# Four changes around the attention layer of a four-layer graph network: where skip terms, keys and row sums are kept and when they move

## The chip, the cores and the metric

The kernel runs on one core of one Trainium2 chip. The metric is the time of one execution on the device in microseconds (us), from the first to the last instruction; the number given for a kernel is the median of several executions. Engines are named as in the profile: PE is the matrix engine, PEld its weight loads, DVE the vector engine, ACT the scalar engine, POOL the general-purpose engine, SP the engine that here only starts transfers. DMA stands for the 16 transfer engines that the core's queues share.

## The reference, cut to what matters

Four graph layers follow one another on 4096 nodes with 128 features each, all with the same dense 4096 x 4096 matrix `adj` of zeros and ones (about 64 ones in a row). After each layer, `x = layernorm(x + layer(x, adj))`. The change concerns the second, an attention with four heads of 32 channels, gated with a linear skip term:

```python
def _L1_gnn_ref(x, adj, Wq, bq, Wk, bk, Wv, bv, Ws, bs, Wb):   # H = 4 heads, C = 32
    q = (x @ Wq + bq).reshape(n, H, C)
    k = (x @ Wk + bk).reshape(n, H, C)
    v = (x @ Wv + bv).reshape(n, H, C)
    attn = jnp.einsum('nhc,mhc->hnm', q, k) / np.float32(np.sqrt(C))
    neg = jnp.where((adj == 0.0)[None], -jnp.inf, attn)
    e = jnp.where(mask[None], 0.0, jnp.exp(neg - m))             # m: row maximum
    alpha = e / denom
    out = jnp.einsum('hnm,mhc->hnc', alpha, v)                   # then transposed to (n, C*H)
    x_r = x @ Ws + bs                                            # the skip term
    beta = jax.nn.sigmoid(jnp.concatenate([out, x_r, out - x_r], axis=-1) @ Wb)
    return beta * x_r + (1.0 - beta) * out
```

The third layer needs the row sums of `adj` (the degrees): `deg = jnp.sum(adj_hat, axis=1)`. The kernel computes them during the second layer, in time that ACT has left there.

## The kernel before

The first layer writes the transposed matrix to DRAM as `adjT`, in 8 x 8 tiles of 128 x 4 x 512 numbers (1 MB each). The second layer has a preparation and a loop.

The preparation makes q and k, 512 nodes at a time. Each is split into a rounded part and a rest (`cut`), written to the DRAM tensor `qk`, and read back into another arrangement of partitions: `KS` for all keys, `QS` for 512 queries. `stack` issues these reads from POOL, four of 256 KB for each piece of 512 nodes. Then the values (`V`, a view of `VA`) and the skip terms get their biases.

```python
            rd = self.dram.tile([P, NT, D], F32, tag="rd", name="rd")
            ...
            def stack(a, dst, c):
                for r, part in enumerate(((0, 1, 0, 1), (0, 0, 1, 1))[a]):
                    nc.gpsimd.dma_start(out=dst[r * C : (r + 1) * C, :, :],
                        in_=qk[a, part, :, c * S : (c + 1) * S].rearrange("(h c) n -> c h n", h=NH))
            ...
                for c in range(NC):                              # 8 pieces
                    for a, w, bias in ((1, wk, bkc), (0, wq, bqc)):
                        p = self.ps_t.tile([P, S], F32, tag="pt", name="pqk")
                        nc.tensor.matmul(p, lhsT=w, rhs=XT[:, s], start=True, stop=True)
                        cut = rot.tile([P, 2, S], F32R, tag="cut", name="cut", bufs=9)
                        nc.scalar.activation(cut[:, 0, :], p, AF.Identity, bias=bias)         # L822
                        nc.vector.scalar_tensor_tensor(cut[:, 1, :], p, bias, ...)            # L823
                        nc.vector.tensor_reduce(mx[:, a, c : c + 1], ...)                     # L826
                        nc.sync.dma_start(out=qk[a, :, :, s]..., in_=cut.bitcast(F32))        # L829
                        if c < 2:
                            stack(a, (QS[c], KS[:, :, s])[a], c)
                for g in self.groups():                          # 8 groups of 4 row blocks: values
                    ...
                    for k, t in enumerate(g):
                        nc.vector.tensor_tensor(V[:, t, :, 0:C], p[:, k, :]..., bvr..., ALU.add)   # L837
                for g in self.groups():                          # skip terms
                    ...
                    r = rot.tile([P, 4, D], F32, tag="r", name="r", bufs=4)
                    nc.vector.tensor_tensor(r, p, bsr.unsqueeze(1).to_broadcast([P, 4, D]), ALU.add)  # L848
                    nc.sync.dma_start(out=rd[:, g[0] : g[-1] + 1, :], in_=r)                  # L849
                ...                                              # a bound on |q||k| -> fi
            small = nc.values_load(fi, min_val=0, max_val=1)
            with tc.If(small > 0) as cmp:
                self.attention_unshifted(VA, KS, QS, at0, stack, rd, wb)   # taken with these inputs
```

The loop runs over 8 tiles of 512 queries (`I`), and in each over 32 blocks of 128 keys (`jb`). One block is four score matmuls (`scores`: PE L909, ACT exponential L916, DVE mask L918) and, two blocks later in the program, eight PE instructions that sum values (`sums`: L935). `load` fetches an `adjT` tile for every four blocks. `row` fetches half a row block of `adj` (1 MB) into the single buffer `nat`, and `degree` sums it along the row on ACT and fetches the next. `ending` finishes a query tile during the first blocks of the next.

```python
            rot = ctx.enter_context(tc.tile_pool(name="rotf", bufs=1))
            atp = ctx.enter_context(tc.tile_pool(name="atf", bufs=2))
            ep = ctx.enter_context(tc.tile_pool(name="ef", bufs=3))
            ...
            def degree(n):
                i, k = halves[n]
                nat = st["nat"]
                nc.scalar.activation(nat, nat, AF.Identity, accum_out=self.deg2[:, k, i : i + 1])  # L901
                row(n + 1)                                       # L894, issued by ACT
            ...
                load(0, 1)
                row(0)
                for n in range(-LEAD, len(seq)):                 # LEAD = 2
                    if n + LEAD < len(seq):
                        I, jb = seq[n + LEAD]
                        if jb % 4 == 0:
                            ...
                                load(m // NT, m % NT // 4)
                        if jb % 4 == 3:
                            degree(8 * I + jb // 4)
                        if I == 0 and jb % 4 == 0 and jb // 4 + 2 < NS:
                            c = jb // 4 + 2
                            stack(1, KS[:, :, c * S : (c + 1) * S], c)
                        if jb == 3 and 0 < I < NS - 1:
                            stack(0, QS[(I + 1) % 2], I + 1)
                        scores(I, jb)
                    if n >= 0:
                        I, jb = seq[n]
                        sums(I, jb)
                        next(rest, None)                         # a step of ending(I - 1)
```

Of the kernel before, what the change touches and what calls it, by code (L numbers as in the profile page):

```python
# [9 lines left out]
F32 = mybir.dt.float32  # L10
F32R = mybir.dt.float32r
AF = mybir.ActivationFunctionType
ALU = mybir.AluOpType
# [3 lines left out]
P = 128  # L17
# [7 lines left out]
S = 512  # L25
# [5 lines left out]
class Net:  # L31
# [3 lines left out]
    def __init__(self, ctx, tc, x, adj):  # L35
        self.tc, self.nc, self.adj = tc, tc.nc, adj
        self.N, self.D = x.shape
        self.NT = self.N // P
        self.MM = min(512, self.N)
        self.const = ctx.enter_context(tc.tile_pool(name="const", bufs=1))  # L40
        self.feat = ctx.enter_context(tc.tile_pool(name="feat", bufs=1))
        self.wtp = ctx.enter_context(tc.tile_pool(name="wtp", bufs=3))
        self.ident = self.const.tile([P, P], F32, tag="ident", name="ident")
        make_identity(self.nc, self.ident)

        self.XA = self.feat.tile([P, self.NT, self.D + 1], F32, tag="X", name="X")
# [722 lines left out]
    def layer1(self, Wq, bq, Wk, bk, Wv, bv, Ws, bs, Wb):  # L769
# [3 lines left out]
        NH, C = 4, D // 4  # L773
        with ExitStack() as ctx:
# [10 lines left out]
            qk = self.dram.tile([2, 2, P, N], F32, tag="qk", name="qk")  # L785
            rd = self.dram.tile([P, NT, D], F32, tag="rd", name="rd")
            wb = [self.load_row(Wb[k * D : (k + 1) * D, 0], f"wb{k}") for k in range(3)]
# [17 lines left out]
            with ExitStack() as pctx:  # L805
# [10 lines left out]
                for c in range(NC):  # L816
                    s = slice(c * S, (c + 1) * S)
                    for a, w, bias in ((1, wk, bkc), (0, wq, bqc)):
                        p = self.ps_t.tile([P, S], F32, tag="pt", name="pqk")
                        nc.tensor.matmul(p, lhsT=w, rhs=XT[:, s], start=True, stop=True)  # L820
                        cut = rot.tile([P, 2, S], F32R, tag="cut", name="cut", bufs=9)
                        nc.scalar.activation(cut[:, 0, :], p, AF.Identity, bias=bias)  # L822
# [9 lines left out]
                for g in self.groups():  # L832
                    p = self.ps_t.tile([P, 4, P], F32, tag="pt", name="pt")
                    for k, t in enumerate(g):
                        nc.tensor.matmul(p[:, k, :], lhsT=XT[:, t * P : (t + 1) * P], rhs=wv, start=True, stop=True)
                    for k, t in enumerate(g):
                        nc.vector.tensor_tensor(  # L837
                            V[:, t, :, 0:C],
                            p[:, k, :].rearrange("p (h c) -> p h c", h=NH),
                            bvr.rearrange("p (h c) -> p h c", h=NH),  # L840
                            ALU.add,
                        )
                for g in self.groups():
                    p = self.ps_t.tile([P, 4, P], F32, tag="pt", name="pt")
                    for k, t in enumerate(g):
                        nc.tensor.matmul(p[:, k, :], lhsT=XT[:, t * P : (t + 1) * P], rhs=ws, start=True, stop=True)
                    r = rot.tile([P, 4, D], F32, tag="r", name="r", bufs=4)
                    nc.vector.tensor_tensor(r, p, bsr.unsqueeze(1).to_broadcast([P, 4, D]), ALU.add)  # L848
                    nc.sync.dma_start(out=rd[:, g[0] : g[-1] + 1, :], in_=r)  # L849

# [13 lines left out]
            with tc.If(small > 0) as cmp:  # L864
                self.attention_unshifted(VA, KS, QS, at0, stack, rd, wb)
            with cmp.Else():
                self.attention_shifted(V, qk, rd, wb)

    def attention_unshifted(self, VA, KS, QS, at0, stack, rd, wb):

# [3 lines left out]
        with ExitStack() as ctx:  # L874
            rot = ctx.enter_context(tc.tile_pool(name="rotf", bufs=1))
            atp = ctx.enter_context(tc.tile_pool(name="atf", bufs=2))
            ep = ctx.enter_context(tc.tile_pool(name="ef", bufs=3))
            ps_s = ctx.enter_context(tc.tile_pool(name="ps_s", bufs=3, space=PSUM))
            ps_v = ctx.enter_context(tc.tile_pool(name="ps_v", bufs=1, space=PSUM))
            st = {("at", 0, 0): at0}  # L880

            def load(I, J):
                at = atp.tile([P, 4, S], F32, tag="at", name="at")
                nc.sync.dma_start(out=at, in_=self.adjT[I, J])
                st["at", I, J] = at

            halves = [(i, k) for i in range(NT) for k in range(2)]

            def row(n):

                if n < len(halves):
                    i, k = halves[n]
                    st["nat"] = rot.tile([P, N // 2], F32, tag="nat", name="nat")
                    nc.scalar.dma_start(  # L894
                        out=st["nat"], in_=self.adj[i * P : (i + 1) * P, k * N // 2 : (k + 1) * N // 2]
                    )

            def degree(n):
                i, k = halves[n]
# [44 lines left out]
            def ending(I):  # L944

                ev = rot.tile([P, 2, S], F32, tag="ev", name="ev")
                for a in range(2):
                    nc.scalar.copy(ev[:, a, :], st["po"][a])
                r = rot.tile([P, 4, D], F32, tag="r", name="r")
                o = rot.tile([P, 4, D], F32, tag="o", name="o")  # L950
# [3 lines left out]
                yield  # L954
                nc.sync.dma_start(out=r, in_=rd[:, 4 * I : 4 * I + 4, :])
                for a in range(2):
# [48 lines left out]
            with tc.manual_schedule():  # L1005
# [3 lines left out]
                for n in range(-LEAD, len(seq)):  # L1009
# [26 lines left out]

    def attention_shifted(self, V, qk, rd, wb):

# [3 lines left out]
        with ExitStack() as ctx:  # L1042
# [3 lines left out]
            KT = keep.tile([P, N], F32, tag="KT", name="KT")  # L1046
            K2 = keep.tile([P, S], F32, tag="K2", name="K2")
            for c in range(N // S):
# [8 lines left out]
            nc.gpsimd.memset(QH, 0.0)  # L1057
            Q2 = keep.tile([P, 2, P], F32, tag="Q2", name="Q2")
            work = ctx.enter_context(tc.tile_pool(name="work1", bufs=1))
            self.on_scalar = 0  # L1060

            for i in range(NT):
# [56 lines left out]
                o = self.wtp.tile([P, D], F32, tag="o", name="o")  # L1119
                r = self.wtp.tile([P, D], F32, tag="r", name="r")  # L1120
                nc.sync.dma_start(out=r, in_=rd[:, i, :])
                nc.scalar.copy(junk[:, 2, :], po)
# [326 lines left out]
```

## Time and profile before

| | |
|---|---|
| time, median of 3 executions | 2413.66 us (2411.61 to 2417.61) |
| profiled execution, span | 2421.0 us |
| mean granted PE clock | 0.912 |
| busy: PE, DVE, ACT, POOL | 84%, 79%, 60%, 4% of the span |
| HBM read, written | 371.20 MB, 79.72 MB |
| first layer (from the timeline) | up to about 981 us |
| second layer, preparation | about 981 to 1031 us |
| second layer, loop | about 1031 to 1875 us |
| third and fourth layers | about 1875 us to the end |

The profile is of one execution. Busy time counts an engine's instructions, not the starting of transfers. The windows view gives, for stretches of the span, each engine's busy time with its number of instructions, then the granted PE clock (1.00 is full speed), the busy share of the DMA engines (it can pass 1 where transfers of several queues overlap) and the rate in GB/s. The waits view lists who waited for whom: total us, number of times, the longest one. The chain is followed back from the last instruction, at each step to what released it; its lines give start, length and what it was. The timeline gives start, length, engine, line and operation, with the idle time before it in brackets. A line such as L916 is a line of the kernel.

### The profile page before, as it was taken

How to read it: one execution, taken by the hardware profiler on the slowest of the kernel's cores; microseconds unless marked ns; L12 is line 12 of the kernel's file. 1: busy time of each engine (PE TensorE's matmuls, PEld its weight loads, DVE VectorE, ACT ScalarE, POOL GpSimd, SP SyncE). 2: the span in 40 equal slices, each digit the busy share in tenths (PEclk: the TensorE clock that was granted, in tenths of full speed). 3: DMA queues.
4: the chain of work that ended last, by engine and by line, in shares of the span. 5: the costliest groups of instructions: out<-in, count | busy, mean ns of one | idle time of the engine just before them, and what ended most of it. 6: DMA issues, size and time to landing. Idle time of an engine off the chain costs nothing.

```text
span 2421.0 us, 24184 instructions
## 1 busy us (share of the span) xinstructions
PE 2028.3 (84%) x8795; PEld 1117.9 (46%) x8795; DVE 1900.7 (79%) x2719; ACT 1459.7 (60%) x1761; POOL 100.7 (4%) x141
## 2 busy tenths in 40 slices
PE   5477878778777771789999999999997899979998
PEld 4266666566666660433333333333332444444443
DVE  6478788788788888757877878878787877568887
ACT  5688888898888886368777787877775000010000
POOL 2000000000000042210000000000000000000000
PEclk7689889889898885789999999999999899979999
DMA  2456465464646530796464655646444788528884
GB/s 53 134 181 204 146 204 199 159 207 154 203 170 191 190 111 1 264 245 200 163 195 143 194 170 166 195 164 187 160 166 171 280 290 284 187 110 294 287 288 169
DMA packets 115174, 452.66 MB, mean 187 GB/s; under 512 B 10016, under 2 KB 20320, under 8 KB 74080
## 3 DMA queue, kind: packets, MB, share of 16 engines
q1 hardware_dynamic: 87248, 298.90, 36.4%
q10 hardware_dynamic: 18576, 135.27, 16.0%
q0 software_dynamic: 9216, 16.78, 3.9%
q8 instruction: 73, 1.20, 0.2%
q14 instruction: 61, 0.50, 0.1%
HBM read 371.20 MB, written 79.72 MB: 186 GB/s over the span
## 4 chain that ended last, share of the span: by engine, by line
PE 56%; DVE 25%; ACT 12%; DMA 3%; issue 3%; ACTq 0%; SPq 0%; POOL 0%; DVEq 0%; POOLq 0%
PE pv L935 14%; PE pa L1324 9%; PE pa L1179 9%; PE ps L909 8%; DVE e L918 5%; PE pz L583 4%; DVE w L606 3%; PE pi L674 3%; DVE t L632 3%; DVE w L636 3%; PE ptA L564 3%; ACT t L628 3%; ACT at L572 2%; ACT e L916 2%; DMA nat<-in_adj_dram 2%
## 5 line engine op out<-in xcount | busy, mean ns | idle before, releaser
L918 DVE SCALAR_TENSOR_TENSOR e<-at,e 128x2048 f32<-128x2048 f32 x256 | 581.4, 2287 | 183.1 <-ACT e L916 183.1
L916 ACT ACTIVATE e<-ps 128x1024 f32<-128x1024 f32 x512 | 489.3, 1025 | 137.5 <-PE ps L909 102.7
L935 PE MATMUL pv<-e,VA 128*64 128x512 f32 x2048 | 505.9, 616 | 7.8 <-DVE e L918 7.5
L909 PE MATMUL ps<-QS,KS 128*128 128x512 f32 x1024 | 317.4, 429 | 41.5 <-ACT e L916 32.9
L909 PEld LDWEIGHTS ps<-QS,KS 128*128 128x128 f32 x1024 | 173.3, 191 | 270.8 <-ACT e L916 177.1
L674 PE MATMUL pi<-HA,w 128*128 128x129 f32 x1152 | 184.6, 334 | 84.1 <-DVE w L636 84.1
L935 PEld LDWEIGHTS pv<-e,VA 128*64 128x64 f32 x2048 | 126.6, 138 | 256.2 <-issue 230.3
L1324 PE MATMUL pa<-w,F 128*128 128x512 f32 x512 | 224.0, 598 | 13.3 <-DVE w L1321 13.3
L1179 PE MATMUL pa<-at,Y 128*128 128x512 f32 x512 | 223.0, 596 | 0.0
L674 PEld LDWEIGHTS pi<-HA,w 128*128 128x128 f32 x1152 | 177.7, 247 | 94.3 <-DVE w L636 94.3
L1321 DVE SCALAR_TENSOR_TENSOR w<-rho,col,at 128x512 f32<-128x512 f32 x256 | 186.7, 746 | 19.7 <-PE pa L1324 2.5
L591 DVE SCALAR_TENSOR_TENSOR t<-ei,de,pz 128x512 f32<-128x512 f32 x144 | 107.3, 747 | 111.4 <-PE pz L583 107.9
L564 PE MATMUL ptA<-ident,ad 128*128 128x128 f32 x1032 | 146.6, 288 | 41.4 <-ACT at L572 34.0
L1189 DVE SCALAR_TENSOR_TENSOR odd<-at 128x2048 f32<-128x2048 f32 x64 | 146.6, 2290 | 38.2 <-DMA at<-adjT 37.6
L564 PEld LDWEIGHTS ptA<-ident,ad 128*128 128x128 f32 x1032 | 125.7, 149 | 99.1 <-ACT at L572 51.3
L572 ACT COPY at<-ptA 128x512 f32<-128x512 f32 x200 | 108.4, 587 | 103.1 <-PE ptA L564 99.1
L583 PE MATMUL pz<-HT 128*128 128x512 f32 x292 | 166.3, 682 | 4.3 <-DVE w L655 4.0
L1324 PEld LDWEIGHTS pa<-w,F 128*128 128x128 f32 x512 | 97.6, 192 | 135.3 <-issue 100.6
L1179 PEld LDWEIGHTS pa<-at,Y 128*128 128x128 f32 x512 | 97.5, 192 | 119.8 <-issue 118.9
L606 DVE TENSOR_TENSOR w<-w,at 128x2048 f32<-128x2048 f32 x64 | 143.7, 2281 | 0.0
L1328 ACT COPY a<-pa 128x512 f32<-128x512 f32 x8 | 4.7, 586 | 206.8 <-PE pa L1324 206.8
L901 ACT ACTIVATE nat<-nat 128x2048 f32<-128x2048 f32 x64 | 122.7, 1918 | 11.1 <-DMA nat<-in_adj_dram 11.1
(340 smaller groups left out, 2370.0 us busy)
## 6 DMA issues: line engine op xcount, KB each, us to landing
at<-adjT SPq DMA_DIRECT2D x127, 1024.0 KB, 4.8
at<-adjT ACTq DMA_DIRECT2D x65, 1024.0 KB, 4.8
ad<-in_adj_dram SPq DMA_DIRECT2D x64, 1024.0 KB, 6.5
adjT<-at SPq DMA_DIRECT2D x64, 1024.0 KB, 8.4
nat<-in_adj_dram ACTq DMA_DIRECT2D x64, 1024.0 KB, 4.9
qk<-cut SPq DMA_DIRECT2D x16, 512.0 KB, 13.3
KS<-qk POOLq DMA_DIRECT2D x32, 256.0 KB, 11.1
QS<-qk POOLq DMA_DIRECT2D x32, 256.0 KB, 8.7
```

The costliest lines, as they stand in the source:

```text
L564: nc.tensor.transpose(pt[:, ib, :], st[p]["ad"][k][:, ib, jb * P : (jb + 1) * P], self.ident)
L572: copy(st[p]["at"][k][:, jb, :], st[p]["pt"].pop(m))
L583: nc.tensor.matmul(pz, lhsT=HT[:, j * P : (j + 1) * P], rhs=HT[:, I * S : (I + 1) * S], start=True, stop=True)
L606: nc.vector.tensor_tensor(w, w, at, ALU.mult)
L674: nc.tensor.matmul(self.po[ib // 2][:, ib % 2, :], lhsT=w[0][:, jb, ib * P : (ib + 1) * P], rhs=HA[:, 4 * J + jb, :], start=False, stop=(J ...
L909: nc.tensor.matmul(p[:, h, :], lhsT=KS[:, h2 + h, jb * P : (jb + 1) * P], rhs=QS[I % 2][:, h2 + h, :], start=True, stop=True,)
L916: nc.scalar.activation(e[:, h2 : h2 + 2, :], p, AF.Exp)
L918: nc.vector.scalar_tensor_tensor(e, at[:, jb % 4, :].unsqueeze(1).to_broadcast([P, NH, S]), 0.0, e, op0=ALU.not_equal, op1=ALU.mult,)
L935: nc.tensor.matmul(st["po"][h // 2][g : g + 64, :], lhsT=VA[:, o : o + 64], rhs=e[:, h, :], start=(jb == 0), stop=(jb == NT - 1), skip_gro ...
L1179: nc.tensor.matmul(pa, lhsT=Y[:, 4 * J + jb, :], rhs=at[:, jb, :], start=False, stop=(J == NS - 1 and jb == 3), skip_group_check=True,)
L1321: nc.vector.scalar_tensor_tensor(w, rho[:, I * S : (I + 1) * S], col[:, 0, j : j + 1], at[:, jb, :], op0=ALU.max, op1=ALU.mult)
L1324: nc.tensor.matmul(pa, lhsT=F[:, j, :], rhs=w, start=False, stop=(j == NT - 1), skip_group_check=True)
```

## The change

It has four parts, all in the second layer, and one that makes room for them.

1. **Skip terms stay in SBUF.** The sums of L848 go into a resident tile `R` (16 KB in each partition). The DRAM tensor `rd`, its eight stores and its eight reads go away.
2. **Keys at the pace of the loop.** POOL copies one number of the exponentials of the block before, ahead of each later `stack` call, so that the reads of a piece of keys are issued only when the loop has come that far. Before, POOL issued all of them at once.
3. **Degree sums begin later.** The first is done at block 11 of the first query tile in place of block 3; the two that are left out come in the last query tile, at blocks 13 and 17.
4. **Values' bias by four row blocks.** One DVE instruction over 128 x 512 numbers in place of four over 128 x 128.
5. **Room.** `cut` has 7 buffers for 9, the loop's `adjT` tiles alternate between `at0` and one more buffer (three were in use at the start), and the general pool `wtp` has 2 buffers for 3.

```diff
-        self.wtp = ctx.enter_context(tc.tile_pool(name="wtp", bufs=3))
+        self.wtp = ctx.enter_context(tc.tile_pool(name="wtp", bufs=2))
...
-            rd = self.dram.tile([P, NT, D], F32, tag="rd", name="rd")
+            R = keep.tile([P, NT, D], F32, tag="R", name="R")
...
-                        cut = rot.tile([P, 2, S], F32R, tag="cut", name="cut", bufs=9)
+                        cut = rot.tile([P, 2, S], F32R, tag="cut", name="cut", bufs=7)
...
-                    for k, t in enumerate(g):
-                        nc.vector.tensor_tensor(
-                            V[:, t, :, 0:C],
-                            p[:, k, :].rearrange("p (h c) -> p h c", h=NH),
-                            bvr.rearrange("p (h c) -> p h c", h=NH),
-                            ALU.add,
-                        )
+                    nc.vector.tensor_tensor(
+                        V[:, g[0] : g[-1] + 1, :, 0:C],
+                        p.rearrange("p t (h c) -> p t h c", h=NH),
+                        bvr.rearrange("p (h c) -> p h c", h=NH).unsqueeze(1).to_broadcast([P, 4, NH, C]),
+                        ALU.add,
+                    )
...
-                    r = rot.tile([P, 4, D], F32, tag="r", name="r", bufs=4)
-                    nc.vector.tensor_tensor(r, p, bsr.unsqueeze(1).to_broadcast([P, 4, D]), ALU.add)
-                    nc.sync.dma_start(out=rd[:, g[0] : g[-1] + 1, :], in_=r)
+                    nc.vector.tensor_tensor(
+                        R[:, g[0] : g[-1] + 1, :], p, bsr.unsqueeze(1).to_broadcast([P, 4, D]), ALU.add
+                    )
...
-            atp = ctx.enter_context(tc.tile_pool(name="atf", bufs=2))
+            atp = ctx.enter_context(tc.tile_pool(name="atf", bufs=1))
...
+            ats = at0, atp.tile([P, 4, S], F32, tag="at", name="at")
+            pace = rot.tile([1, 1], F32, tag="pace", name="pace")

             def load(I, J):
-                at = atp.tile([P, 4, S], F32, tag="at", name="at")
+                at = st["at", I, J] = ats[J % 2]
                 nc.sync.dma_start(out=at, in_=self.adjT[I, J])
-                st["at", I, J] = at
...
-                r = rot.tile([P, 4, D], F32, tag="r", name="r")
+                r = R[:, 4 * I : 4 * I + 4, :]
...
-                nc.sync.dma_start(out=r, in_=rd[:, 4 * I : 4 * I + 4, :])
...
-                        if jb % 4 == 3:
-                            degree(8 * I + jb // 4)
+                        if jb % 4 == 3 and (I or jb > 8) or I == NS - 1 and jb in (13, 17):
+                            degree()
                         if I == 0 and jb % 4 == 0 and jb // 4 + 2 < NS:
                             c = jb // 4 + 2
+                            if jb:
+                                nc.gpsimd.tensor_copy(pace, st["e", I, jb - 1][0:1, 0, 0:1])
                             stack(1, KS[:, :, c * S : (c + 1) * S], c)
```

`degree()` now takes its number from the row that was fetched last. The other branch of the `If` (`attention_shifted`), which these inputs don't take, is adapted to the same tiles.

More of the change, by code (lines that the diff above doesn't have):

```diff
@@ L864, in layer1, with attention_unshifted @@
             with tc.If(small > 0) as cmp:
-                self.attention_unshifted(VA, KS, QS, at0, stack, rd, wb)
+                self.attention_unshifted(VA, KS, QS, at0, stack, R, wb)
             with cmp.Else():
-                self.attention_shifted(V, qk, rd, wb)
-    def attention_unshifted(self, VA, KS, QS, at0, stack, rd, wb):
+                self.attention_shifted(V, qk, R, wb, at0)
+    def attention_unshifted(self, VA, KS, QS, at0, stack, R, wb):
         nc, tc, N, NT, NS, D, X = self.nc, self.tc, self.N, self.NT, self.NS, self.D, self.X
@@ L892, in row @@
                     i, k = halves[n]
+                    st["row"] = n
                     st["nat"] = rot.tile([P, N // 2], F32, tag="nat", name="nat")
@@ L896, in row, with degree @@
                     )
-            def degree(n):
+            def degree():
+                n = st["row"]
                 i, k = halves[n]
@@ L1035, in attention_unshifted, with attention_shifted @@
             nc.vector.tensor_tensor(self.deg, self.deg2[:, 0, :], self.deg2[:, 1, :], ALU.add)
-    def attention_shifted(self, V, qk, rd, wb):
+    def attention_shifted(self, V, qk, R, wb, spare):
         nc, tc, N, NT, D, X = self.nc, self.tc, self.N, self.NT, self.D, self.X
@@ L1046, in attention_shifted @@
             KT = keep.tile([P, N], F32, tag="KT", name="KT")
-            K2 = keep.tile([P, S], F32, tag="K2", name="K2")
+            K2, Q2 = spare[:, 0, :], spare[:, 1, 0 : 2 * P].rearrange("p (k n) -> p k n", k=2)
             for c in range(N // S):
@@ L1057, in attention_shifted @@
             nc.gpsimd.memset(QH, 0.0)
-            Q2 = keep.tile([P, 2, P], F32, tag="Q2", name="Q2")
             work = ctx.enter_context(tc.tile_pool(name="work1", bufs=1))
@@ L1119, in attention_shifted @@
                 o = self.wtp.tile([P, D], F32, tag="o", name="o")
-                r = self.wtp.tile([P, D], F32, tag="r", name="r")
-                nc.sync.dma_start(out=r, in_=rd[:, i, :])
+                r = R[:, i, :]
                 nc.scalar.copy(junk[:, 2, :], po)
```

## The prediction

> **What bounds the kernel now.** I read the page's first lines, then the windows, to see whether the second layer's loop has a pace of its own.
>
> ```profile
> PE 2028.3 (84%) x8795; PEld 1117.9 (46%) x8795; DVE 1900.7 (79%) x2719; ACT 1459.7 (60%) x1761; POOL 100.7 (4%) x141
> ```
>
> ```profile
> 1031.00:1162.00 131.00, 121.00 (x470) 46.77 (x470) 91.31 (x63) 96.72 (x103) 10.32 (x19) 0.94 0.82 215
> 1162.00:1265.00 103.00, 99.20 (x395) 38.15 (x394) 82.08 (x86) 77.86 (x87) 2.16 (x4) 0.98 0.55 177
> ...
> 1677.00:1780.00 103.00, 99.17 (x394) 38.34 (x394) 81.99 (x85) 78.05 (x86) 0.00 (x0) 0.98 0.47 167
> ```
>
> Whole-span shares tell little: the four layers differ. The windows are cut where the same mask instruction comes round in each query tile. From the second tile on each takes 103 us with PE busy for 99; ACT and DVE have 20 us and more to spare. So the loop is PE's: in the timeline, blocks follow each other at 2.99 us (1078.5 to 1108.5 us, ten blocks in 30 us), and nothing taken off ACT, DVE or the transfers speeds that up. What can be had lies where PE stands still, before and at the start of the loop. The chain of waits there:
>
> ```profile
> 993.48 12.54 DMA qk<-cut
> ...
> 1008.18 6.33 DVE VA L837 x32
> 1014.51 0.61 DVE r L848
> ...
> 1015.14 7.73 DMA rd<-r
> ...
> 1025.55 4.97 DMA rd<-r
> ...
> 1030.62 15.52 DMA nat<-in_adj_dram
> 1046.16 2.01 ACT nat L901 x2
> ...
> 1048.19 12.34 DMA nat<-in_adj_dram
> ...
> 1062.59 10.68 DMA nat<-in_adj_dram
> 1073.29 2.01 ACT nat L901 x2
> ```
>
> From 993 to 1073 us the chain consists mostly of transfers: the stores of q and k, two stores of skip terms, three reads of half rows for the degree sums. The waits over 960 to 1090 us say how much an engine lost to each:
>
> ```profile
> ACT nat L901 <- DMA nat<-in_adj_dram: 11.1, 3, 9.5
> ...
> ACT cut L822 <- DMA qk<-cut: 6.9, 4, 2.2
> ...
> ACT e L916 <- DMA rd<-r: 5.5, 1, 5.5
> DVE r L848 <- DMA rd<-r: 5.2, 1, 5.2
> ```
>
> The reader should see the difference: the chain shows 15.52 + 12.34 + 10.68 = 38.5 us in half rows, but ACT stood idle for only 11.1 us of it, since exponentials were done meanwhile. The second view counts.
>
> **What the skill says.** "DMA: Bandwidth & Descriptors", section "Issuing engines are not separate DMA queues": transfers started by the scalar, sync and general-purpose engines run on the same 16 engines and interleave. The trace agrees: the half row issued at 1030.6 us lands after 15.5 us while POOL pours in 24 key reads and two `adjT` tiles; the 58 issued after 1100 us take 4.9 us at the median. "TensorE: Matmul & The Clock Gate", section "What's actually happening": an idle window of about 3.4 us halves PE's clock, and a busy one restores it. In the windows 1020 to 1026 and 1044 to 1050 us, where PE hardly works, the granted clock is 0.50, and 1.00 from 1056 us on. So a PE stall here costs somewhat more than itself. "VectorE: DVE Perf Modes", section on the errata: a fixed cost for each instruction, so that many small tiles pay it often. Agrees: an L837 of 128 x 128 takes 277 ns, an L848 of 128 x 512 only 677 ns.
>
> **Part by part.**
>
> *Values' bias.* 32 instructions fill 6.41 us (a pitch of 0.20). Eight of 128 x 512 from PSUM should run as L848 does in sequence (four in 2.47 us, a pitch of 0.62): 8 x 0.62 = 5.0. Gain 1.4 us, on the chain.
>
> *Skip terms in SBUF.* The first four L848 run from 1014.44 us, then DVE waits 5.2 us for a store to free a buffer; the last ends at 1025.5. Without stores all eight need 5.0 us. Then ACT's first exponential waits 5.5 us more, to 1031.05, since its tile lies where `r` lay and the last store lands at 1030.5. Both waits go. Reads of `r` inside the loop are hidden (landing 1140.35 + 9 us at most, first used at 1155), worth nothing.
>
> *Seven cut buffers.* This costs. ACT's timeline shows the rhythm: cut 12 starts at 995.36, cut 13 at 998.21, cut 14 at 1000.83, cut 16 at 1006.12 us, each when the store nine cuts earlier has landed, some 2.6 us apart. With seven, cut 16 waits for store 9 in place of 7. Two stores further at 2.4 us: it starts at about 1010.8, 4.7 us later. DVE's last cut work (0.75 + 0.67) then ends near 1012.6 (before: 1008.2), unless value additions slip in between.
>
> *The start of the loop.* Before: the bound `fi` at 1023.6, PE's first score at 1025.95, ACT at 1031.05. After: 1012.6 + 5.0 (values) + 5.0 (skip terms) = 1022.6; `fi` can come a little ahead of the last skip terms, say 1021.5. PE follows 2.4 us later, and the first two score matmuls at half clock need 1.6 us: the first exponential at 1025.5. Gain 5.5 us. The stores of q and k (8.4 MB) and the early stacks (4.2 MB) at the 380 GB/s of 996 to 1014 us take 33 us from about 989, until 1022, so they set no later limit.
>
> *Degree sums later, keys paced.* L935 groups in the timeline give the progress: block 0 at 1035.48, block 10 at 1077.50, 42.0 us for what takes 10 x 2.99 = 29.9 at full pace. Some 2.6 us of the 12.1 are PE's cold start and stay (an estimate: six score matmuls at up to 792 ns against 389 at full clock). With the first degree sum at block 11, the row has over 25 us to land: 9.5 us gained. Each degree sum still takes 2.5 us of ACT (1841.84 to 1844.31 below, the issue in it), but ACT has about 1 us to spare in a block. Against it: key reads now meet the half rows of blocks 11 to 23. A 1 MB piece of keys takes some 5.4 us of all 16 engines (10.49 MB fill 44.0% of 122 us), an `adjT` tile and a half row 2.7 each at 380 GB/s; 10.8 us in every 12. I allow 1 us of new waits.
>
> *Two more sums in the last tile.* At blocks 11, 13, 15, 17 and 19 they come every two blocks, 5.98 us, with one `nat` buffer.
>
> ```profile
> 1841.84 1.92 ACT L901 ACTIVATE nat<-nat 128x2048 f32<-128x2048 f32 x1
> 1843.64 0.20 ACT L901 ACTIVATION_READ_ACCUMULATOR nat<-nat 128x1 f32 x1
> 1843.88 0.33 ACTq L894 DMA_DIRECT2D nat<-in_adj_dram  x1
> 1844.31 3.77 ACT L916 ACTIVATE e<-ps 128x1024 f32<-128x1024 f32 x4 [0.47 <-DVE e L918]
> ```
>
> The next row is issued 2.04 us after a sum starts and lands 4.9 us later, so sums can't be closer than 7.0 us; where an `adjT` tile comes at the same time (after 13 and 17) landing takes 6.2 (6.6 was seen beside two others), so 8.3. Four intervals: 2 x 7.0 + 2 x 8.3 = 30.6 for 23.9, 6.7 us late. A block's exponentials are ready some 2 us before PE needs them, which is taken off: a loss of 4.5 us.
>
> *The rest.* One POOL copy of one number, five times, and pool `wtp` with two buffers: in the timeline the third user of `rs4` starts after the first one's last reader at 972.03 us (972.75), so I count 0.
>
> Sum: -5.5 - 9.5 + 1 + 4.5 = -9.5. From 2413.7: **2404 us**.
>
> **Rivals.**
>
> *A: the chain is right, the whole of the transfers goes.* 38.5 + 12.7 us would make 2363, faster by 2.1%. For it: the chain's words. Against: the waits (11.1 + 10.7), and PE's pace in the same stretch. The whole distance to full pace is 12 us. I give it little.
>
> *B: the tail eats the gain.* If the five close sums stall ACT for full landings, or `adjT` tiles fall in with each, 8 to 10 us are lost instead of 4.5, and with seven cut buffers the loop starts no earlier than before: about 2413 to 2416. For it: every second of the four intervals meets an `adjT` tile. Against: exponentials run two blocks ahead, and after block 19 ACT has four blocks to catch up in.
>
> *C: PE becomes free earlier than I count.* If value additions are done while DVE waits for the last cuts (it idles 2.6 us between 1002 and 1008), the loop starts at about 1021, and with the warmer PE 16 to 19 us come in place of 9.5: 2395 to 2398.
>
> **Range and chances.** Between C's 2395 and B's 2414 I set the range 2395 to 2413; the executions before spread by 6 us, a third of it. Two per cent are 48 us: neither rival reaches that on the slow side, and only A on the fast one. Chances: faster by over 2% 0.02, within 0.96, slower 0.02.
>
> **What will show it.** Right: no wait of ACT L901 for `nat` in the first tile, the first exponential at about 1025.5, block 10 some 15 us earlier than 1077.5, later tiles still 103 us, and in the last tile new ACT waits for `nat` of 4 to 7 us. Wrong: waits for `cut` that grow beyond 12 us, key reads that PE waits for, a last tile as fast as before, or a change outside the second layer, which would point to tiles that now lie elsewhere.

## The result, and the profile after

The changed kernel takes **2402.09 us** (median of 4 executions, 2399.93 to 2406.34), the kernel before, run beside it, 2415.64 us. The ratio is 0.9943, with a 95% interval of 0.9915 to 0.9972: some 13.5 us less, between 7 and 21. It lies inside the predicted range, 2 us under the predicted 2404.

The first line of the page of the changed kernel answers to the one shown of before:

```profile
PE 2018.2 (84%) x8795; PEld 1117.5 (47%) x8795; DVE 1901.2 (79%) x2695; ACT 1459.8 (61%) x1761; POOL 107.1 (4%) x146
```

PE executes the same 8795 instructions and is busy for 10 us less: not less work, but more of it at full clock (0.918 granted on average, 0.912 before). DVE lost 24 instructions, which are 32 value additions turned into 8; POOL gained the five pacing copies. First comes a window of the kernel before that covers most of its blocks 0 to 10, then windows of the changed kernel, cut at block 0 and block 10 of the first query tile, and from the first ending's gate exponential to the next one's (columns: stretch, length, then busy us and count of PE, PEld, DVE, ACT, POOL, then PE clock, DMA share, GB/s):

```profile
1031.00:1073.00 42.00, 32.49 (x112) 12.19 (x113) 23.11 (x11) 24.91 (x26) 8.15 (x15) 0.81 1.32 277
```

```profile
1026.40:1056.30 29.90, 29.89 (x120) 11.65 (x120) 22.65 (x10) 20.53 (x23) 4.64 (x10) 1.00 0.90 189
...
1146.10:1249.00 102.90, 99.11 (x393) 38.16 (x394) 82.03 (x86) 77.70 (x85) 2.14 (x4) 0.98 0.54 174
```

Blocks 0 to 10 now take 29.9 us with PE busy in all of it at a clock of 1.00; before it was 42.0 us, and in the window shown PE was busy for 32.5 of 42.0 us at a clock of 0.81. A later query tile takes 103 us, as before. The waits over the same 960 to 1090 us as in the prediction (who waited, for what: total us, times, longest):

```profile
POOL pace L1024 <- DVE e L920: 47.4, 5, 11.0
...
DVE cut L823 <- ACT cut L822: 12.1, 8, 3.0
...
ACT cut L822 <- DMA qk<-cut: 10.3, 5, 2.4
...
ACT nat L903 <- DMA nat<-in_adj_dram: 0.3, 1, 0.3
```

The 11.1 us that ACT lost to half rows are 0.3, and both waits for `rd` are gone. POOL's new wait of 47.4 us is the intended pacing; PE, busy without a pause over blocks 0 to 10, loses nothing to it there. ACT's wait for a free `cut` buffer has grown from 6.9 to 10.3 us. The preparation's end in the timeline of the changed kernel (start, length, engine, line, operation, count, and in brackets the idle time before):

```profile
1007.61 2.07 PE L835 MATMUL pt<-wv,XT 128*128 128x128 f32 x8 [1.01 <-DVE cut L823]
1008.06 4.86 DVE L836 TENSOR_TENSOR VA<-pt,bvr 128x512 f32<-128x512 f32 x8
...
1009.47 7.85 PE L845 MATMUL pt<-ws,XT 128*128 128x128 f32 x64
...
1017.36 0.69 DVE L846 TENSOR_TENSOR R<-pt,bsr 128x512 f32<-128x512 f32 x1 [0.20 <-PE pt L845]
...
1021.98 5.61 ACT L918 ACTIVATE e<-ps 128x1024 f32<-128x1024 f32 x6 [1.02 <-PE ps L911]
```

Value additions and skip terms now follow each other on DVE with almost no gap, from 1008.06 to 1018.05 us, and the exponentials start 3.9 us later. A group of eight value matmuls at 1001.87 us takes 1.16 us; the 2.07 us here are PE at about half clock.

Where the profiled time went, in stretches taken from both traces:

| stretch | before, us | after, us | difference |
|---|---|---|---|
| first `cut` to first exponential | 47.7 | 44.4 | -3.3 |
| block 0 to block 10 | 42.0 | 29.9 | -12.1 |
| block 10 to the first ending's gate | 89.7 | 89.8 | +0.1 |
| six query tiles after that | 618.4 | 616.7 | -1.7 |
| last query tile, to its last root | 87.7 | 90.2 | +2.5 |
| last root to the third layer's first large matmul | 13.0 | 16.4 | +3.4 |
| fourth layer, first wide score matmul to first sum | 41.0 | 36.0 | -5.0 |

The spans of the two profiles, 2421.0 and 2398.1 us, differ by more than this (22.9 us). The time up to the first `cut`, which is mostly the first layer, is 983.4 us in one and 977.6 in the other. Over the fourteen profiles of this study it lies between 977 and 984 us, with three `wtp` buffers (979.9 and 983.4) as with two (976.9 to 984.1), so the change is not seen in it. The six query tiles take 615.0 to 618.4 us in these profiles, and their -1.7 is no more than that scatter. So two rows are what the prediction did not have: the third layer starts later, and the fourth layer's preparation is shorter.

### The profile page after: what moved, and what is told of

It reads as the page before. It is cut to its first block, busy times and chain, and to the rows that moved or that the text cites. A ratio compares the mean times of both kernels' runs of the same rounds, so it can differ in the third digit from the quotient of the medians.

```text
span 2398.1 us, 24121 instructions
## 1 busy us (share of the span) xinstructions
PE 2018.2 (84%) x8795; PEld 1117.5 (47%) x8795; DVE 1901.2 (79%) x2695; ACT 1459.8 (61%) x1761; POOL 107.1 (4%) x146
## 4 chain that ended last, share of the span: by engine, by line
PE 56%; DVE 25%; ACT 12%; issue 3%; DMA 2%; ACTq 0%; POOL 0%; SPq 0%; DVEq 0%; POOLq 0%
PE pv L937 15%; PE pa L1327 9%; PE pa L1182 9%; PE ps L911 9%; DVE e L920 5%; PE pz L583 4%; DVE w L606 3%; PE pi L674 3%; DVE w L636 3%; DVE t L632 3%; PE ptA L564 3%; ACT t L628 3%; ACT e L918 2%; ACT at L572 2%; ACT w L601 1%
## 5 line engine op out<-in xcount | busy, mean ns | idle before, releaser
L564 PE MATMUL ptA<-ident,ad 128*128 128x128 f32 x1032 | 145.8, 287 | 41.2 <-ACT at L572 34.1
L583 PE MATMUL pz<-HT 128*128 128x512 f32 x292 | 161.5, 664 | 4.9 <-DVE w L655 4.6
```

Source lines behind the costliest of these rows:

```text
L564: nc.tensor.transpose(pt[:, ib, :], st[p]["ad"][k][:, ib, jb * P : (jb + 1) * P], self.ident)
L583: nc.tensor.matmul(pz, lhsT=HT[:, j * P : (j + 1) * P], rhs=HT[:, I * S : (I + 1) * S], start=True, stop=True)
```

## The experiments

Four things were to be settled. Did the first tile's stall end because the degree sums begin later, or because keys are paced? What do the sums cost in the last tile: their landing, or ACT's own time? Why does the third layer start later? And why did the fourth layer's preparation change? The edits are against the changed kernel unless said otherwise. Each run was timed beside the kernel before on the same chip, and ratios are to that.

### Degree sums from block 3 again, keys paced

```diff
-                        if jb % 4 == 3 and (I or jb > 8) or I == NS - 1 and jb in (13, 17):
+                        if jb % 4 == 3:
```

> The changed kernel with the degree sums where they were before: one in every four blocks from block 3 of the first tile on, none extra in the last tile. Keys are still read at the pace of the loop. Theory A (the prediction's: the sum at block 3 comes too early, whatever else moves): ACT waits for the first half row again by several us (9.5 before), block 0 to block 10 takes 36 to 42 us in place of 29.9, and the last tile gets back its 2.5 us: slower by 4 to 9 us. Theory B (the crowd of key reads made the half row late, and pacing alone cures it): the first half row lands within 8 us, ACT waits under 2 us, block 0 to 10 takes 30 to 32 us, and the kernel is as fast as the changed one or 1 to 3 us faster, because the last tile isn't lengthened.

Measured: 2399.15 us, ratio 0.9932 (0.9916 to 0.9949). Block 0 to 10 takes 30.0 us, with no wait of ACT for a half row in the whole loop, and the last tile 87.7 us, as before. So with paced keys the later start brings nothing, and it costs 2.5 us at the end.

### Later sums, keys not paced

```diff
-                            if jb:
-                                nc.gpsimd.tensor_copy(pace, st["e", I, jb - 1][0:1, 0, 0:1])
```

> The changed kernel without POOL's copies: all 24 remaining key reads are issued at once at the start of the loop, the degree sums still begin at block 11. Theory A: no engine needs the half row before block 11, so the crowd is hidden: block 0 to 10 stays at 30 us, no difference over 2 us. Theory B (the crowd delays the second transposed tile too, which block 4 needs): DVE's masks wait at block 4, block 0 to 10 takes 33 us or more, slower by 3 us or more.

Measured: 2403.44 us, 0.9946 (0.9929 to 0.9964). Block 0 to 10 again takes 30.0 us; the stretch after it 92.1 in place of 89.8. One line of its waits over 1015 to 1165 us says why:

```profile
ACT nat L903 <- DMA nat<-in_adj_dram: 2.6, 1, 2.6
```

The second half row still meets the unpaced keys. The first has time enough. So each of the two cures takes away the stall in the first ten blocks by itself, but later sums alone leave 2.3 us of it for the blocks after.

### Neither of the two

Both edits above together; what is left of the change are the skip terms in SBUF, the values' bias and the room made.

> The changed kernel with neither remedy for the first tile: degree sums from block 3 on, and all later key reads issued at once. Skip terms stay resident. Theory (the crowd of key reads is the whole cause of the first tile's loss, and either remedy alone takes it): block 0 to block 10 goes back to 40 to 42 us, ACT waits some 10 us for half rows; slower than the changed kernel by 8 to 10 us, still 2 to 4 us faster than before. Rival (the skip terms' stores were a good part of the crowd): with them gone the first half row lands within 10 us and block 0 to 10 takes 33 to 36 us.

Measured: 2407.79 us, 0.9961 (0.9948 to 0.9974). Its waits over the same stretch:

```profile
ACT nat L903 <- DMA nat<-in_adj_dram: 7.9, 3, 3.4
```

Block 0 to the first ending's gate takes 34.0 + 94.5 = 128.5 us; before it was 131.7, in the changed kernel 119.7. So 8.8 of the 12.0 us are the crowd of key reads. Pacing alone removes all of them (119.7 us in the run with sums from block 3), later sums alone 6.5 (122.1). The other 3.2 us come with the rest of the change: the first half row is now issued at 1020.3 us, 0.5 us ahead of the first of the later key reads, and lands after 4.8 us; before, ACT could issue it only when the last store of skip terms had landed, 5.8 us behind the first of them, and it took 15.5 us. The kernel before also starts two `adjT` loads there, this one a single one; what each of the two differences is worth was not tried apart.

### The kernel before, with its keys paced and nothing else

The two lines of the pacing copy, and its tile, added to the kernel before.

> The kernel before with POOL's pacing copies alone; skip terms through DRAM, sums from block 3, nine buffers. Theory: block 0 to 10 takes 30 to 31 us in place of 42.0, everything else stays: faster by 11 to 12 us, about 2403. Rival (without room the half row still comes late, since two transposed tiles are fetched at the start): 33 to 36 us, faster by 6 to 9.

Measured: 2408.18 us, 0.9965 (0.9956 to 0.9974). Block 0 to 10 takes 32.0 us in place of 42.0. Its waits over 1015 to 1165 us:

```profile
ACT e L917 <- DMA rd<-r: 5.3, 1, 5.3
DVE r L848 <- DMA rd<-r: 4.3, 1, 4.3
...
ACT nat L902 <- DMA nat<-in_adj_dram: 2.7, 1, 2.7
```

That lies between the 30 to 31 us of the theory and the 33 to 36 of its rival, and the whole kernel gains 8.5 us where 11 to 12 were expected. Five copies of one number take 8.4 us off the waits for half rows (11.1 to 2.7). The two waits for `rd` stay, as they must, since the skip terms still go to DRAM; they are the other half of the change.

### The last tile's sums spread every three blocks

```diff
-                        if jb % 4 == 3 and (I or jb > 8) or I == NS - 1 and jb in (13, 17):
+                        if (jb % 4 == 3 and (jb > 8 or I)) if I < NS - 1 else (jb % 3 == 0 and jb):
```

> The changed kernel with the ten degree sums of the last tile every three blocks (blocks 3, 6, ... 30) in place of 3, 7, 11, 13, 15, 17, 19, 23, 27, 31. Theory: two blocks (5.98 us) are shorter than a half row's round (2.0 us to issue, 4.9 to land), three (8.97) are longer; ACT's waits for half rows in the last tile (2.9 us in three) go, and the last tile, from its first gate exponential to its last root, takes 87.5 us as before the change in place of 90.0: faster by about 2.5 us. Rival (it is ACT's own 2.5 us for each sum, not the landing, that costs): the ten sums still cost, the tile stays at 89 to 90 us.

Measured: 2402.73 us, 0.9950 (0.9934 to 0.9967). The last tile takes 89.8 us, against 90.2 in the changed kernel and 87.7 before. The waits of that tile, first the changed kernel, then the one with spread sums:

```profile
PE ps L911 <- ACT e L918: 5.9, 6, 2.2
...
ACT nat L903 <- DMA nat<-in_adj_dram: 2.9, 3, 1.2
```

```profile
PE ps L911 <- ACT e L918: 5.1, 2, 2.8
```

Without one wait for a half row PE still loses 5.1 us to ACT, where before it lost 3.9. So the landing is not what costs; two more sums of about 2.5 us each are, in both places tried (the tile takes 89.7 to 90.4 us in all five profiles with the changed kernel's own spacing, so the 0.4 us of difference is within their scatter). With the even spacing they fall into the first blocks of the tile, where ACT also has the ending of the tile before; that they collide there is read from this, not tested apart.

### Eight buffers for the cuts

```diff
-                        cut = rot.tile([P, 2, S], F32R, tag="cut", name="cut", bufs=7)
+                        cut = rot.tile([P, 2, S], F32R, tag="cut", name="cut", bufs=8)
```

> The changed kernel with 8 buffers for the pieces of q and k in place of 7. Theory: each buffer is worth one store's distance; the first to the last piece on ACT takes 25.5 to 26 us in place of 28.5 (22.7 with nine), and the first exponential comes 2.5 to 3 us earlier after the first piece (41.5 in place of 44.4). Rival (the stores' total of 12.6 MB sets the start, or PE's cold clock does): the pieces come earlier but the first exponential gains under 1.5 us.

Measured: 2397.54 us, 0.9920 (0.9899 to 0.9942). First to sixteenth `cut` takes 26.5 us with eight buffers, 28.5 with seven, 22.7 with nine (before); the first exponential comes 42.9 us after the first `cut`. In the eight profiles with seven buffers of this study it comes after 43.6 to 46.0 us, in the three with eight after 42.5 to 42.9: a gain of some 1 to 3 us, where 2.5 to 3 were expected.

### The skip terms in a pool of their own

The tile `R` came from the pool of keys and values. The first loads of the third layer are SP's, and the chain shows that start. In the chain of the changed kernel (start, length, what):

```profile
1853.08 5.98 issue
...
1860.23 9.17 DMA at<-adjT
...
1869.45 5.60 PE pa L1182 x7
```

And in that of the kernel before:

```profile
1873.41 3.96 issue
...
1878.50 4.71 DMA at<-adjT
```

ACT's first load of 1 MB lands after 9.17 us in place of 4.71, and it is issued 7.2 us after the last root in place of 5.1. In the chain these 2.1 us are "issue", time for which the profile shows no cause. (Before, a test, a scaling and two small matmuls, 3.2 us in all, still came behind the landing.) SP's waits say what went wrong before it; first the changed kernel over 1780 to 1880 us, then the kernel before over 1800 to 1890:

```profile
SPq L1180 <- DVE X L989: 34.6, 1, 34.6
```

```profile
SPq L1177 <- PE pto L959: 25.0, 1, 25.0
```

Before, SP could start the third layer's first loads once PE had done the last transposes, 10 us ahead of the last root. Now it waits for L989, DVE's last read of `R`, and starts 1.3 us ahead of it. So SP's four loads overlap with ACT's: the last of them lands 14.1 us after the root, in place of 3.8, which was ahead of ACT's first. In the program as built no tile of the third layer lies at the addresses of `R`, so it should be the pool that is released as a whole. To test it:

```diff
+            skip = ctx.enter_context(tc.tile_pool(name="skip1", bufs=1))
+            R = skip.tile([P, NT, D], F32, tag="R", name="R")
...
-            R = keep.tile([P, NT, D], F32, tag="R", name="R")
```

> The changed kernel with the skip tile in a pool of its own, allocated ahead of the pool with keys and values; nothing else. Theory: in the changed kernel the third layer's first loads wait for the last read of the skip tile, because the pool is released as a whole (SP waits for the line that reads it, and issues 4.7 us after the last tile's gate exponential where before it issued 4.1 us ahead of it). Freed, SP issues at about 4 us ahead again, PE's first large matmul of the third layer comes 19 us after that exponential in place of 22.5: faster by 3 to 4 us. Rival: the late loads only collide with ACT's loads by chance of the order; then the distance stays at 22 us.

Measured: 2403.79 us, 0.9948 (0.9932 to 0.9965). SP's loads do start 10.1 us ahead of the last root again, and yet the first large matmul comes 19.7 us after it, later than in either kernel. DVE's timeline tells why:

```profile
1861.26 2.29 DVE L1193 SCALAR_TENSOR_TENSOR odd<-at 128x2048 f32<-128x2048 f32 x1 [5.14 <-DMA at<-adjT]
...
1868.15 6.36 DVE L1166 TENSOR_SCALAR Y<-X,deg 128x128 f32<-128x128 f32 x32
```

Three tests of the matrix (L1193, whether an entry is other than 0 or 1; 2.3 us each) stand ahead of the scaling `Y`, which the matmuls need. Half of the theory held (the pool delays SP), half fell (that this alone brings the time back).

### The scalings held together

Own pool, sums from block 3, and the loop of scalings in a scope that was meant to keep it ahead of the tests:

```diff
+            with tc.manual_schedule():
+                for t in range(NT):
+                    nc.vector.tensor_scalar(Y[:, t, :], X[:, t, :], d[:, t : t + 1], None, op0=ALU.mult)
```

> The changed kernel with the degree sums from block 3 on (none extra in the last tile), the skip tile in a pool of its own, and the third layer's 32 scalings of rows put ahead of its checks of the matrix on DVE. Theory: the skip tile's pool let SP's loads start early, and what ate that gain was three checks (2.3 us each) that went ahead of the scalings; with the order fixed, the first large matmul of the third layer comes 10 to 11 us after the last root of the second in place of 16.4, and with the 2.5 us of the last tile the kernel is 7 to 9 us faster than the changed one: 2393 to 2396. Rival (PE waits for the transposed tiles, not for the scalings): 14 us or more, and only the last tile's 2.5 us are gained.

Measured: 2405.41 us, 0.9952 (0.9932 to 0.9973). DVE's order did not change, three tests still came first, and the stretch is 19.6 us. The run tells nothing about the theory, only that this isn't the means.

### All of it together, the tests bound behind the scalings

Own pool, sums from block 3, eight cut buffers, and a zero that is made from the last scaled column, so that no test can stand ahead of it:

```diff
+            zero = keep.tile([P, 1], F32, tag="zero", name="zerocol")
+            nc.vector.tensor_scalar(zero, Y[:, NT - 1, 0:1], 0.0, None, op0=ALU.mult)
...
-                        odd, at, 0.0, at, op0=ALU.not_equal, op1=ALU.not_equal,
+                        odd, at, zero, at, op0=ALU.not_equal, op1=ALU.not_equal,
```

> The changed kernel with sums from block 3 on, the skip tile in its own pool, 8 buffers for the pieces of q and k, and the third layer's matrix checks on DVE bound behind its scalings through a zero that is computed from the last scaling. Theory: the end of the second layer to the third's first large matmul takes 10 to 11 us in place of 16.4 (it was 19.6 while three checks stood ahead of the scalings), the last tile 87.5 in place of 90.2, the start 1.5 us less: 8 to 10 us faster than the changed kernel, about 2393. Rival (the checks were not what PE waited for, or SP's and ACT's loads collide again): 15 us or more there, 4 us gained in all.

Measured: **2392.37 us, 0.9892 (0.9874 to 0.9910)**, faster than both kernels. The third layer's first large matmul comes 10.3 us after the last root (13.0 before, 16.4 after). In the timeline:

```profile
1855.40 6.36 DVE L1166 TENSOR_SCALAR Y<-X,deg 128x128 f32<-128x128 f32 x32
```

```profile
1859.95 5.49 PE L1185 MATMUL pa<-at,Y 128*128 128x512 f32 x6 [2.12 <-DMA at<-adjT]
```

The scaling now starts at once, and what PE waits for last is a transfer of 4.8 us. The first exponential comes after 42.5 us, the last tile takes 87.7.

### The changed kernel once more

> The changed kernel itself, beside the kernels of this call on one chip, as their measure. Expected by every theory: about 2402 us, 0.994 of the kernel before; block 0 to 10 in 29.9 us, 16 us from the second layer's last root to the third layer's first large matmul, 36 us in the fourth layer's preparation from its first wide score matmul to its first sum.

Measured beside the last one: 2401.70 us, 0.9935 (0.9919 to 0.9951). So the combined kernel gains another 9.3 us on the same chip. Its stretches repeat those of the first profile within 1.6 us: 46.0 (start), 29.9, 89.7, 615.5, 89.9, 16.3 and 36.0 us.

### Queries of the second tile read later

The combined kernel, with the reads of the second tile's queries (1 MB) moved from the preparation to block 23.

> As the combined kernel, and the second query tile's 1 MB is read from block 23 of the first tile on, in place of the preparation. Theory (transfers set the start: stores wait beside reads that nobody needs yet): the pieces of q and k go through ACT 2 to 3 us faster, the first exponential comes 2 to 3 us earlier than in the combined kernel (about 40 us after the first piece); about 2391. Rival (PE's half clock and DVE's additions set the start): under 1 us.

Measured: 2394.30 us, 0.9897 (0.9876 to 0.9918). The start takes 42.5 us in both. Taking a megabyte off the transfers of the preparation brings nothing. From DVE's last work on a `cut` it is 14.8 and 14.7 us to the first exponential. The chain goes there through PE, 2.1 us for the last eight value matmuls and 9.0 for the 64 of the skip terms, the first part at half clock, then the last addition and the bound; no transfer is in it.

### The kernel before with two `wtp` buffers

```diff
-        self.wtp = ctx.enter_context(tc.tile_pool(name="wtp", bufs=3))
+        self.wtp = ctx.enter_context(tc.tile_pool(name="wtp", bufs=2))
```

> The kernel before with the general pool at 2 buffers in place of 3, nothing else. Theory (the smaller pool changes the order in which PE's work of the fourth layer's preparation is laid out, and with it how long PE runs there at half clock): from the first wide score matmul to the first sum 36 us in place of 41.0, the rest of the kernel as before; faster by 4 to 5 us, about 2411 to 2413. Rival (the clock's moment is chance, or the rest of the change sets it): 41 us, no difference over 2 us.

Measured: 2413.81 us, 0.9984 (0.9974 to 0.9994): 3.9 us less, between 1.5 and 6.3. The fourth layer's preparation takes 37.7 us in place of 41.0; the stretches of the second layer stay (47.5, 41.2, 89.7, 87.7). The other profile with three buffers, the kernel before with paced keys, has 41.0 us too. What happens there is seen in PE's timeline of the kernel before, and then of the changed kernel:

```profile
2140.03 2.06 PE L1266 MATMUL psr<-XT,us 128*128 128x512 f32 x2
...
2143.45 6.75 PE L1266 MATMUL psr<-XT,us 128*128 128x512 f32 x8
```

```profile
2124.01 3.68 PE L1269 MATMUL psr<-XT,us 128*128 128x512 f32 x8
```

Eight equal matmuls take 6.75 or 3.68 us. The windows of the kernel before over those microseconds show the clock:

```profile
2135.00:2140.00 5.00, 5.00 (x33) 4.04 (x33) 1.22 (x2) 0.00 (x0) 0.00 (x0) 0.94 0.00 0
2140.00:2145.00 5.00, 5.00 (x13) 3.23 (x14) 1.37 (x4) 0.00 (x0) 0.00 (x0) 0.50 0.00 0
2145.00:2150.00 5.00, 5.00 (x7) 1.69 (x5) 5.00 (x9) 0.00 (x0) 0.00 (x0) 0.54 0.00 0
```

PE is listed as busy for all of each, and the granted clock is 0.94, 0.50 and 0.54: together 10.2 us at half clock, of which half, 5.1, is lost. That is the whole difference of 5.0 us; in the changed kernel the windows from 2115 to 2130 us show 1.00 throughout. With one `wtp` buffer less, transposes and one-column matmuls stand in another order on PE. But the order doesn't settle it: all twelve profiles with two buffers show the same order around there, and it took 36.0 us in seven of them, 37.7 in three, 39.4 in one and 44.3 in one (the own pool alone), the longer the clock was at one half (15, 19.5, 23 and 33 us of the stretch). What makes the clock fall at one moment or another was not found. The reverse, the changed kernel with three buffers, was not run.

## Why the prediction was right, and where its steps were not

**The bound** was read rightly. Later query tiles stay at 103 us, everything gained lies at the start or outside of the loop, and the rival that took the chain's 38.5 us at their word would have made 2363.

**Values' bias:** 8 instructions fill 4.86 us for 6.41, a gain of 1.5 on DVE; predicted 1.4. In the changed kernel the chain leads through PE here (2.07 us of value matmuls, then 7.66 of skip terms), so how much of it reached the first exponential is not shown.

**The start of the loop** was mis-sized: -5.5 us predicted, -3.3 and -1.7 in the two profiles. Two terms were short. The later `cut` was put at 4.7 us; DVE's last work on it ends 5.8 and 6.5 us later, counted from the first `cut`. And from there to the first exponential I had 12.9 us (1012.6 to 1025.5), where it took 13.8 and 14.7. The additions take 10.0 us from first to last in the first profile, as predicted; but `fi` comes behind the last of the skip terms and not ahead of it, 10.9 us after the last `cut` in place of 8.9, while the way from `fi` on was 3.0 us in place of 4.0. The last 0.9 us of the second profile are a cold PE: the skip terms' 64 matmuls take 9.15 us there, 7.85 in the first, and DVE waits 0.2 us ahead of each of its last five additions. While ACT and DVE wait for stores, PE stands still for 0.4 to 1.7 us between its groups of eight. "TensorE: Matmul & The Clock Gate", section "Loop structure matters more than you think", says that a long wait ahead of each matmul lets PE go cold, with 8 us as its example. The trace agrees that waits do it, though here a row of these short ones was enough (2.07 us for a group against 1.16). With eight buffers nearly the whole predicted gain arrives (42.5 to 42.9 us for 47.7).

**Block 0 to 10:** -9.5 predicted, -12.1 measured. The term that failed is the cold PE: I left 2.6 us in the stretch as something that stays. The first cold start lies ahead of block 0 (4.4 us from the first exponential to block 0, in both), and the later ones came from the stalls and went with them. The cause was right, the crowd on the transfer engines, and the way out was not as I told it: I booked the gain under later sums with room to land, but pacing alone does it (the run with sums from block 3; in the kernel before, 10.0 us of it). The +1 us of new waits was 0: 0.3 us in the first tile.

**The last tile:** +4.5 predicted, +2.5 measured, and for another reason. I made the loss from landings (7.0 and 8.3 us between sums); the waits for half rows come to 2.9 us, and taking all of them away changes the tile by 0.4 us. What is left as the cost is ACT's own time, which I had called spare; PE loses 5.1 us to ACT's exponentials without any such wait, for 3.9 before. The rival of a tail that eats the whole gain fell with this.

**Not counted at all:** the later third layer, +3.4 us, from a tile that holds its pool open; and the fourth layer's preparation, -5.0 us in the profile and some 4 timed for `wtp` alone, which I had put at 0. I named the sign ("a change outside the second layer") and did not think of what a released pool sets free.

**The sum.** Start, block 0 to 10, last tile and third layer make -3.3 - 12.1 + 2.5 + 3.4 = -9.5 us, the predicted number, out of terms of which each is off by 2 to 3.4 us. With -5.0 of the fourth layer it is -14.5, beside 13.5 timed. So direction and size are right for the reason given, waits for stores and half rows at the loop's start, and the closeness of the sum is partly luck: errors of opposite sign. The rival of a PE that comes free earlier named a time (2395 to 2398) near the measured one, but its mechanism did not occur: no value addition stands ahead of the last `cut` on DVE.

**The signs.** Counted from the first `cut`, block 10 came 15.4 us earlier (15 forecast), and later tiles kept their 103 us. The new waits for half rows in the last tile stayed under the forecast, 2.9 us for 4 to 7.

**Left open:** why PE's clock falls in the fourth layer at one moment or another, and what the order of its instructions has to do with it; how much of the first tile's 3.2 us is the skip terms' and how much the one load of `adjT` less; and how the preparation would fare with nine buffers, which was not tried in the changed kernel.

## What to carry to other kernels

Where a burst of transfers that is needed only later crowds out one that is needed now, let its issuer read something small from the loop before each piece: here five copies of one number took most of the stall away, and holding back the consumer as well brought nothing more. When a tile becomes resident, ask which pool it holds open, since the next stage's first loads can hang on its last reader. And when a start gets faster, look at what an engine's queue then puts first: the own pool lost time until the tests were bound behind the work that PE waits for.

## What the runs showed of the hardware

PE can fall to half clock while its record has no gap: in the kernel before, at 2140 us, 13 instructions fill a window of 5.00 us at a clock of 0.50, in a stretch where matmuls of one column stand between the large ones. "TensorE: Matmul & The Clock Gate", section "What's actually happening", ties the clock to how busy PE has lately been; that this view's busy time isn't that measure is what I had not expected. (The ends of matmuls are modelled in this view, so it may hide gaps.) And no long wait is needed for half clock: in the preparation groups of eight matmuls took 2.07 us for 1.16 in a row of waits of 0.4 to 1.7 us. But single waits as long left it at full clock (1.8 and 1.2 us in the kernel before, both followed by 1.16 us), so these runs give no limit.
